# Attention with a gated feed-forward block: where the first sequence's loads stand among the next sequence's moments, and which engine empties its value sums

## The chip, the cores and the metric

The kernel runs on one core of one Trainium2 chip. A core has a matrix engine (TensorE, PE in the profile, with its weight loads as PEld), a vector engine (VectorE, DVE), an activation engine (ScalarE, ACT), a general engine (GpSimd, POOL) and a queue engine that issues transfers (SyncE, SP). The metric is the device time of one launch in microseconds (us). Three runs of the kernel before gave 599.13, 599.91 and 601.34 us; the median is 599.91 us.

## The reference, cut to what matters

Eight sequences of 512 positions and 256 features go through a layer norm, then through two branches whose results are multiplied: attention with 16 heads of 16 features, rotary positions and a causal window of 250 positions, and a three-layer network whose weights are only signs.

```python
xn = _layernorm(x, axis=-1)
# attention
proj = xn @ in_proj_w.T                      # q, k, v
q, k = _apply_rope(q, k)
mask = (delta >= 0) & (delta < CONTEXT)      # CONTEXT = 250
scores = einsum('bhtd,bhsd->bhts', q, k) * D ** (-0.5)
attn = softmax(where(mask, scores, finfo.min))
s = einsum('bhts,bhsd->bhtd', attn, v).reshape(B, T, E) @ out_proj_w.T
# feed-forward with weights of +1 and -1
h = relu(s0 * conn(k0, concat([xn, -xn]))) * 2
h = relu(s1 * conn(k1, h)) * 2
g = silu(s2 * conn(k2, h))
x = x + s * g
```

## The kernel before, in words

The program goes through the sequences b = 0 to 7 and overlaps them: while PE works on the network of sequence b, the attention of b and the projections of b + 1 are put between its matmuls. Every piece of work has a planned place, a number in a planner's time in which each sequence has 42 units (`SEQ = 42.0`). The pieces are sorted by that number and issued in that order (`run`, line 234); a piece can return follow-ups with a delay. The order is then fixed: each engine carries out its instructions in just this order. The same holds for SP: a transfer whose condition is not met holds up every transfer behind it.

The pieces that the change and the prediction touch:

- **Queries and keys to DRAM.** After projection and rotation, `split_hi` and `split_lo` (lines 431 and 437) write a high and a low part of keys and queries to the DRAM tiles `dk` and `dq` (`to_dram`, line 427). Each part is 512 KB and is written twice.
- **Stacks.** `stack(b, g)` (line 444) reads them back for one group g of four heads (g = 0 to 3): four loads of 256 KB, `k` pair 0, `q` pair 0, `k` pair 1, `q` pair 1 (line 450). Loads of `q` need all writes of `dq` to have landed.
- **Moments of the next sequence.** Means and scales of the 512 positions of b + 1 are computed on DVE and POOL (`stats`, line 253), turned by DVE and written to a small DRAM tile `d` by four transfers of 1 KB (`lay_down`, line 289). `load_xT` (line 281) loads the transposed input, 512 KB. `lay_over` (line 298) reads `d` back, broadcast to all 128 partitions, as `of_all`, 512 KB; it can only be issued when the four small writes have landed. `norm_turned` (line 309) then normalises the transposed input in four DVE instructions, two for each half c, and the projection `ka` (line 381) of b + 1 needs its result, the first half of `ka` the half c = 0, the second c = 1.
- **Attention steps.** Two groups take three steps (0 to 2 for groups 0 and 1, 3 to 5 for groups 2 and 3). `step` issues twelve score matmuls into six PSUM banks `sc` (line 746), then the value matmuls of the step before into `po` (line 828), and lets ACT take the exponentials `p` (line 771) and POOL mask them (lines 791 and 798). Step 0 uses group 0 alone: four matmuls with the loads of pair 0, then four with pair 1, then four with both. Step 1 needs group 1 as well, from its third matmul on; pair 1 of group 1 from its seventh.
- **Value sums.** When a group is done, `keep` (line 839) takes its sums out of PSUM: twice for an even group (`V` with a mask, and `S`, both ACT), twice for an odd group (both DVE). There is a single `po` buffer, so the next group's first value matmul waits for this.

In `attention`, the place of the stacks of groups 0 and 1 is fixed relative to `first`, the planned start of the attention, 24.7 for sequence 0. Before, both groups stand at 24.7 - 7.6 = 17.1. The moments of sequence 1 stand at 16.9 (`lay_down`), 17.15 (`load_xT`) and 17.2 (`lay_over`).

Of the kernel before, what the change touches and what calls it, by code (L numbers as in the profile page):

```python
# [16 lines left out]
ALU = mybir.AluOpType  # L17
# [17 lines left out]
def tile_attention_times_gated_ffn(  # L35
# [42 lines left out]
    nc = tc.nc  # L78
# [42 lines left out]
    first_half, second_half = s_sb[:, 3:4], s_sb[:, 4:5]  # L121
# [322 lines left out]
    def stack(b, g):  # L444
        st = states[b]
        for pair in range(2):
            for what in "kq":
                t = stacks.tile([P, T], F32R, tag=f"{what}{pair}", name=f"{what}_{b}_{g}_{pair}")
                rows = st["dram", what][ds(32 * g + 16 * pair, 16)]
                nc.sync.dma_start(t.bitcast(F32), rows.rearrange("p n t -> (p n) t"))  # L450
                st[what, g, pair] = t
# [358 lines left out]
    def values(b, i, tiles):  # L810

        st = states[b]
        blocks = [(*x[:4], tiles, *x[4:]) for x in steps[i]]
        g = over[0][0] if over else blocks[0][0]
        assert over or i == 0 or st["group"] == g or blocks[0][1:3] == (0, 0)
        now = [x for x in over + blocks if x[0] == g]
        now.sort(key=lambda x: x[1:3] != (0, 0))
        if not now:
            return
        over[:] = [x for x in blocks if x[0] != g]  # L820
        if now[0][1:3] == (0, 0):
            st["po"] = ps_o.tile([P, T], F32, tag="po", name=f"po_{b}_{g}")
            st["group"] = g
        po = st["po"]
        done = i >= used[g][-1]
        for k, (_, j, first, n, tiles_, y, off) in enumerate(now):
            for r in range(4):
                nc.tensor.matmul(  # L828
                    po[32 * r : 32 * r + 32, ds(j * P + first, n)],
                    v_columns(j, g, r),  # L830
                    place(tiles_, r, y, off, n),
                    start=(j == 0),
                    stop=(done and k == len(now) - 1),
                    skip_group_check=True,
                )
        if done:
            return [(0.0, lambda: keep(b, g, po))]

    def keep(b, g, po):

        st = states[b]
        odd = g % 2
        S = st["S", g] = outs.tile([P, T], F32, tag="S", name=f"S_{b}_{g}", bufs=3)
        if odd:
            V = st["V", g // 2]
            nc.vector.scalar_tensor_tensor(V, po, second_half, V, ALU.mult, ALU.add)
            nc.vector.tensor_copy(S, po)
        else:
            V = st["V", g // 2] = outs.tile(
                [P, T], F32, tag=f"V{g // 2}", name=f"V_{b}_{g}", bufs=2  # L850
            )
            nc.scalar.mul(V, po, first_half)
            nc.scalar.copy(S, po)

    def flush():
        if pending:
# [4 lines left out]
    def step(b, i):  # L861
        sc = scores(b, i)
        had = len(pending)
        more = flush() or []
        tiles, exps, rest = exponentials(b, i, sc)
        pending.append((rest, (b, i, tiles)))
        return [(-1.4 if had else 0.0, exps)] + more

    def attention(b, among):

        first, end = SEQ * b + (24.7 if b == 0 else 0.0), ends_at(b)
        inside = sorted((at, cost) for at, cost, _ in among if first <= at < end)
        whole = sum(cost for _, cost in inside)
        times, done = [], 0.0
        places = {}
        for at, cost in inside:
            if at in quick or b == 0 and at not in inner:
                places[at] = done
            done += cost
        for n in range(len(steps)):  # L880
            at = min(places, key=lambda at: abs(places[at] * len(steps) - whole * n))
            del places[at]
            times.append(at - 0.01)
        out = []
        for n in range(len(steps)):
            out.append((times[n], 2.5, lambda n=n: step(b, n)))
        for g in range(NG):

            at = times[used[g - 2][-1]] + 0.01 if g > 1 else first - (
                7.6 if b == 0 else 4.0 if b == 1 else 9.0  # L890
            )
            if b and g == 3:
                at += 5.0
            if b and g == 1:
                at = first + 0.01
            out.append((at, 0, lambda g=g: stack(b, g)))
        if b + 1 == B:
            out.append((end, 0.7, flush))
        return out

    def ends_at(b):
        return SEQ * b + (33.0 if b + 1 == B else SEQ)
# [158 lines left out]
    for b in range(B):  # L1061
# [4 lines left out]
        for t in range(NT):  # L1066
            if b + 1 < B:
                at = SEQ * b + 1.5 if b else 2.0
                everything.append((at + t, 0, lambda b=b, t=t: load_x(b + 1, t)))
        everything += divisions(b) + finish(b, b + 1 == B)  # L1070
    for b in range(B):
        everything += attention(b, everything)
# [54 lines left out]
    with tc.If(found < n_rows, label="general"):  # L1127
        for b in range(B):
            for t in range(NT):
                load_x(b, t)  # L1130
            run(prepare(b, plain=True))
            plain_ffn(b)
            for u in range(len(outputs(b))):
                run(finish_ffn(b, u, "at once"))
            for g in range(NG):
                stack(b, g)
                po = ps_o.tile([P, T], F32, tag="po", name=f"f_po_{b}_{g}")
                for t in range(NT):
                    for r in range(4):
                        shifted(b, g, t, r, po)  # L1140
                keep(b, g, po)
                if g % 2:
                    run(divisions(b, (g // 2,)))
            run(finish(b))
# [59 lines left out]
```

## Time and profile before

| what | value |
| --- | --- |
| median of three runs | 599.91 us (599.13 to 601.34) |
| time of the profiled execution | 598.2 us |
| its span, first to last instruction | 596.5 us |
| mean granted TensorE clock | 0.999 |
| PE busy | 584.8 us, 98% of the span |
| DVE, ACT, POOL busy | 333.7, 303.0, 269.9 us (56, 51, 45%) |
| matmuls of the network, L511, share of the chain that ended last | 44% |
| all PE work in that chain | 88% |

The profile is read from PE. The chain of work that ended last is PE work for 88% of the span, so the time is the sum of the matmuls and of the short gaps between them. A gap in PE's timeline that no later wait swallows is a part of the time; everything on another engine counts only where PE, or something that ends in PE, waits for it.

Before the attention of sequence 0 starts, some 37 us into the span, the program loads weights, normalises sequence 0 and sends its keys and queries through DRAM.

### The profile page before, as it was taken

The page shows a single profiled execution, that of the slowest core. Times are in us where ns is not written, and L with a number is a line of the kernel's source. Part 1 is how long each engine was busy: PE and PEld are TensorE (multiplying, and loading weights), DVE is VectorE, ACT ScalarE, POOL GpSimd, SP SyncE. Part 2 cuts the span into 40 slices and gives each one's busy share as a digit, 9 for nine tenths or more (in the row PEclk, how much of TensorE's full clock was granted, in tenths as well). Part 3 has the DMA queues.
Part 4 walks back from the last instruction along what each step waited for, and adds up shares of the span by engine and source line. Part 5 has one row for each costly group of instructions (what it writes and reads, how often), then busy time and mean ns, then how long its engine had stood idle before and what let it go on. Part 6 is the DMA issues. An engine that isn't in the chain of part 4 may idle for free.

```text
span 596.5 us, 10410 instructions
## 1 busy us (share of the span) xinstructions
PE 584.8 (98%) x3788; PEld 364.7 (61%) x3788; DVE 333.7 (56%) x578; ACT 303.0 (51%) x571; POOL 269.9 (45%) x474
## 2 busy tenths in 40 slices
PE   7999999999999999999999999999999999999996
PEld 6655565655655556555566556665566555657785
DVE  6936335666346754478436684366744666427256
ACT  4747564545464545536454465544644645465422
POOL 2736533436334552445444355333652437435513
PEclk9999999999999999999999999999999999999999
DMA  9764844337432474415654075441673335441111
GB/s 277 283 234 143 294 152 127 108 141 250 146 117 98 170 240 133 147 65 223 208 165 154 2 293 189 130 142 65 238 228 113 107 135 208 158 143 43 35 28 53
DMA packets 50086, 92.24 MB, mean 155 GB/s; under 512 B 10992, under 2 KB 18672, under 8 KB 50032
## 3 DMA queue, kind: packets, MB, share of 16 engines
q1 hardware_dynamic: 47600, 89.31, 44.1%
q10 hardware_dynamic: 2432, 2.23, 1.2%
q8 instruction: 31, 0.51, 0.3%
q14 instruction: 23, 0.19, 0.1%
HBM read 53.22 MB, written 38.30 MB: 153 GB/s over the span
## 4 chain that ended last, share of the span: by engine, by line
PE 88%; DVE 3%; DMA 3%; ACT 2%; SPq 1%; POOL 1%; issue 1%; DVEq 0%; POOLq 0%; ACTq 0%
PE h_ps L511 44%; PE po L828 11%; PE z_ps L562 9%; PE sc L746 7%; PE v_ps L361 4%; PE att_ps L962 4%; PE ka_ps L381 2%; PE qb_ps L381 2%; PE qa_ps L381 2%; PE kb_ps L381 2%; DMA of_all<-d 1%; DMA dq<-m_qa 1%; PE warm L232 1%; SPq L450 1%; DMA dk<-kh 1%
## 5 line engine op out<-in xcount | busy, mean ns | idle before, releaser
L771 ACT ACTIVATE p<-sc 128x512 f32<-128x512 f32 (+2 forms) x288 | 150.2, 607 | 57.6 <-PE sc L746 57.4
L791 POOL TENSOR_SCALAR_AFFINE_SELECT p<-p 128x256 f32<-128x256 f32 (+1 forms) x224 | 104.8, 479 | 123.1 <-ACT p L771 105.4
L511 PE MATMUL h_ps<-h1l,w_sb 128*128 128x512 f32 (+1 forms) x576 | 145.3, 394 | 0.0
L511 PE MATMUL h_ps<-h1h,w_sb 128*128 128x512 f16 (+1 forms) x576 | 123.1, 356 | 0.0
L511 PEld LDWEIGHTS h_ps<-h1l,w_sb 128*128 128x128 f32 x576 | 100.4, 188 | 27.4 <-issue 5.7
L511 PEld LDWEIGHTS <-w_sb 128*128 128x128 f16 x704 | 61.3, 98 | 86.3 <-issue 41.5
L522 ACT ACTIVATE h2h<-h_ps 128x512 f16<-128x512 f32 (+1 forms) x72 | 39.6, 550 | 133.1 <-PE h_ps L511 133.1
L520 DVE SCALAR_TENSOR_TENSOR h2l<-h_ps,h2h 128x512 fp32r<-128x512 f32 (+1 forms) x72 | 44.8, 622 | 93.9 <-ACT h2h L522 93.4
L828 PE MATMUL po<-p,v_pad 128*32 128x378 f32 (+4 forms) x1152 | 71.5, 380 | 0.0
L520 DVE SCALAR_TENSOR_TENSOR h1l<-h_ps,h1h 128x512 fp32r<-128x512 f32 x64 | 43.2, 688 | 45.3 <-ACT h1h L522 45.1
L798 POOL TENSOR_SCALAR_AFFINE_SELECT p<-p 128x256 f32<-128x256 f32 x144 | 57.5, 399 | 0.3 <-POOL p L791 0.3
L746 PEld LDWEIGHTS sc<-q,k 64*128 64x128 f32 x576 | 41.9, 186 | 25.0 <-issue 15.1
L633 DVE RECIPROCAL den<-den 128x256 f32<-128x256 f32 (+1 forms) x32 | 52.4, 1641 | 3.7 <-ACT den L628 3.7
L746 PE MATMUL sc<-q,k 64*128 64x378 f32 (+4 forms) x576 | 52.2, 310 | 2.2 <-ACT p L771 1.2
L522 ACT ACTIVATE h1h<-h_ps 128x512 f16<-128x512 f32 x64 | 37.6, 603 | 30.0 <-PE h_ps L511 30.0
L511 PE MATMUL h_ps<-xl,w_sb 128*128 128x512 f32 x128 | 52.3, 489 | 0.0
L952 POOL TENSOR_TENSOR V<-V,R 128x512 f32<-128x512 f32 x16 | 21.2, 1327 | 52.4 <-DVE R L951 52.4
L828 PEld LDWEIGHTS po<-p,v_pad 128*32 128x32 f32 x1152 | 30.7, 109 | 21.2 <-issue 12.0
L991 POOL TENSOR_TENSOR gate<-gate,xr 128x512 f32<-128x512 f32 (+1 forms) x15 | 18.6, 1242 | 47.6 <-DVE gate L984 26.6
L418 POOL TENSOR_TENSOR m_qa<-m_qa,m_qb 128x512 f32<-128x512 f32 x16 | 21.1, 1343 | 38.5 <-DVE m_qb L397 38.5
L511 PE MATMUL h_ps<-xh,w_sb 128*128 128x512 f16 x128 | 38.5, 383 | 0.0
L562 PE MATMUL z_ps<-h2l,w_sb 128*128 128x512 f32 (+1 forms) x144 | 35.6, 389 | 0.0
(102 smaller groups left out, 656.9 us busy)
## 6 DMA issues: line engine op xcount, KB each, us to landing
k<-dk SPq DMA_DIRECT2D x64, 256.0 KB
q<-dq SPq DMA_DIRECT2D x64, 256.0 KB
dk<-kh SPq DMA_DIRECT2D x16, 512.0 KB
dk<-m_ka SPq DMA_DIRECT2D x16, 512.0 KB
dq<-qh SPq DMA_DIRECT2D x16, 512.0 KB
dq<-m_qa SPq DMA_DIRECT2D x16, 512.0 KB
x<-in_x_dram SPq DMA_DIRECT2D x30, 128.0 KB
xT<-in_x_t_dram SPq DMA_DIRECT2D x7, 512.0 KB
```

Source lines behind the costliest of these rows:

```text
L361: nc.tensor.matmul(v.rearrange("p n s d -> p (n s d)"), st["xT"][:, c, ts(t, P)], wqkv_sb[:, c, 2 * E :], start=(c == 0), stop=(c == EC - 1),)
L381: nc.tensor.matmul(ps[:, cols], wqkv_sb[:, c, ds(col, P)], st["xT"][:, c, cols], start=(c == 0), stop=(c == EC - 1),)
L511: nc.tensor.matmul(ph, weights(w, p, c, ts(f, P)), st[src + p][:, c, cols], start=(k == 0), stop=(k == n - 1),)
L520: nc.vector.scalar_tensor_tensor(lo, ph, 0.0, hi, ALU.max, ALU.subtract)
L522: high = lambda: nc.scalar.activation(hi, ph, AF.Relu)
L562: nc.tensor.matmul(pz, weights(w2, p, c, ts(f, P)), st["h2" + p][:, c, cols], start=(c == 0 and p == "h"), stop=(c == NF1 - 1 and p == "l"),)
L633: nc.vector.reciprocal(part, part)
L746: nc.tensor.matmul(sc[r + (4 if y else 2 * pair)][:, ds(at, n)], st["k", g, pair][row, ts(j, P)], st["q", g, pair][row, ds(j * P + first, n)],
L771: nc.scalar.activation(p, s_, AF.Exp, scale=D ** -0.5)
L791: nc.gpsimd.affine_select(out=block, in_=block, compare_op=ALU.is_ge, fill=0.0, base=0, pattern=[[0, heads], [1, P]], channel_multiplier=-1,)
L798: nc.gpsimd.affine_select(out=block, in_=block, compare_op=ALU.is_ge, fill=0.0, base=-1, pattern=[[0, heads], [-1, beyond]], channel_multi ...
L828: nc.tensor.matmul(po[32 * r : 32 * r + 32, ds(j * P + first, n)], v_columns(j, g, r), place(tiles_, r, y, off, n), start=(j == 0), stop=( ...
```

## The change

Two edits, both for sequence 0 alone. In `attention`, the stacks of group 0 move from 17.1 to 24.7 - 7.9 = 16.8, and those of group 1 to 16.8 + 0.5 = 17.3. In `keep`, the two instructions that take an even group out of PSUM are written by DVE in place of ACT; there are two even groups in a sequence, 0 and 2. Nothing is computed differently.

```diff
@@ -849,8 +849,12 @@
             V = st["V", g // 2] = outs.tile(
                 [P, T], F32, tag=f"V{g // 2}", name=f"V_{b}_{g}", bufs=2
             )
-            nc.scalar.mul(V, po, first_half)
-            nc.scalar.copy(S, po)
+            if b == 0:
+                nc.vector.tensor_scalar(V, po, first_half, None, ALU.mult)
+                nc.vector.tensor_copy(S, po)
+            else:
+                nc.scalar.mul(V, po, first_half)
+                nc.scalar.copy(S, po)
 
@@ -887,12 +891,12 @@
             at = times[used[g - 2][-1]] + 0.01 if g > 1 else first - (
-                7.6 if b == 0 else 4.0 if b == 1 else 9.0
+                7.9 if b == 0 else 4.0 if b == 1 else 9.0
             )
             if b and g == 3:
                 at += 5.0
-            if b and g == 1:
-                at = first + 0.01
+            if g == 1:
+                at = first + 0.01 if b else at + 0.5
             out.append((at, 0, lambda g=g: stack(b, g)))
```

On SP the order of these transfers was: four writes of `d`, four loads of group 0, four loads of group 1, `xT`, `of_all`. It becomes: four loads of group 0, four writes of `d`, `xT`, `of_all`, four loads of group 1. The orders of PE and POOL are as before; ACT has four instructions fewer, DVE four more, each pair on DVE standing between two instructions that were there before (the first between line 397 of `m_kb` and line 441 of `m_ka`, the second between two of line 520). Sequences 1 to 7 keep their order on every engine.

## The prediction

> **What bounds the kernel now.** I read first the waits of PE over the whole span, since PE is busy for 98% of it. An engine, its line, whom it waited for, us in total, times, longest:
>
> ```profile
> PE sc L746 <- ACT p L771: 1.2, 1, 1.2
> PE sc L746 <- DMA q<-dq: 1.0, 1, 1.0
> PE ka_ps L381 <- ACT xT L344: 0.5, 1, 0.5
> PE z_ps L562 <- ACT h2h L522: 0.4, 1, 0.4
> PE ka_ps L381 <- DVE xT L309: 0.2, 1, 0.2
> ```
>
> Beside these there is only a start-up wait of 2.8 us. So no change in transfers can win more than a few us. The next view is PE's timeline where the first and the last of these lie (start, length, instruction, idle time before):
>
> ```profile
> 37.56 0.50 PE L746 MATMUL sc<-q,k 64*128 64x378 f32 x4
> 39.26 0.79 PE L746 MATMUL sc<-q,k 64*128 64x378 f32 x8 [1.20 <-ACT p L771]
> 39.98 1.90 PE L511 MATMUL h_ps<-h1h,w_sb 128*128 128x512 f16 x8
> ...
> 43.66 1.08 PE L746 MATMUL sc<-q,k 64*128 64x378 f32 x12
> 44.67 1.49 PE L828 MATMUL po<-p,v_pad 128*32 128x378 f32 x24
> 46.21 1.10 PE L381 MATMUL ka_ps<-xT,wqkv_sb 128*128 128x512 f32 x2
> 47.50 1.12 PE L381 MATMUL ka_ps<-xT,wqkv_sb 128*128 128x512 f32 x2 [0.19 <-DVE xT L309]
> ```
>
> This is sequence 0: step 0 stops after four of its twelve matmuls, and `ka` of sequence 1 stops between its halves. Third, SP's timeline before it:
>
> ```profile
> 26.37 1.28 SPq L427 DMA_DIRECT2D dq<-m_qa  x2
> 31.85 1.33 SPq L289 DMA_DIRECT2D d<-moments  x4
> 33.23 0.35 SPq L450 DMA_DIRECT2D k<-dk  x1
> ...
> 37.00 0.38 SPq L281 DMA_DIRECT2D xT<-in_x_t_dram  x1
> 37.43 0.60 SPq L298 DMA_DIRECT2D of_all<-d  x1
> ```
>
> The stacks stand behind d, which SP can't issue before the moments are turned at 31.82. In between the transfer engines are nearly idle: the stretches of half a microsecond show 393 GB/s to 30.5, then 49 GB/s and less until bytes of the stacks flow from 34.25 on.
>
> The 1.2 us are put down to ACT, which I don't believe. The exponentials that ended at 39.23 read the two banks that the first four matmuls filled; the fifth goes to a third bank, whose former user ended by 26.9 (the copy of v, L368). In the compiled order this matmul also waits for pair 1 of group 0, whose q was issued at 34.58. Landing at 39.2 would be 4.6 us after its issue; four loads of group 1 press in behind it. The lines below show 3.35 us for a like load.
>
> **The change part by part.**
>
> *Stacks of group 0 earlier.* When dq has landed comes from the next sequence, where q is held up by just that:
>
> ```profile
> 74.71 0.32 SPq L450 DMA_DIRECT2D q<-dq  x1
> 75.08 0.42 SPq L450 DMA_DIRECT2D k<-dk  x1
> 75.55 0.43 SPq L450 DMA_DIRECT2D q<-dq  x1
> 76.02 1.58 SPq L918 DMA_DIRECT2D dsums<-S  x2
> 79.21 0.34 SPq L926 DMA_DIRECT2D sums<-dsums  x1
> ```
>
> The chain of waits has dq<-m_qa landing at 74.64 there, some 0.65 us after its last bytes (about 74.0, the rest being the first k). In sequence 0 the last bytes pass at 30.55, so dq lands at 31.2. Bounds: not before 30.55, not after 33.69, when q was issued without a wait. I take 31.2, as its row is the same transfer. The first k needs dk alone and goes out at once behind dq. Then q, k, q at 31.2, 31.6 and 32.0; the last lands 3.35 us (78.90 less 75.55) to 4.66 us (above) later, at 35.4 to 36.7. Step 0 needs it at 37.8, so its wait is gone. Without it the twelve matmuls take 1.00 us (43.66 to 44.67) instead of 2.42 (37.56 to 39.98): 1.42 us. But h_ps of f = 3 takes the bank that the first exponential frees, which ends at 38.73, against 38.56 for the last score; with some 0.06 us of signalling PE goes on at 38.8. **Gain 1.18 us**, and step 1 begins at 42.48.
>
> *d, xT and of_all behind the stacks.* d follows at 32.5 (four issues in 1.33 us, to 33.8). The nearest row for a small write behind three stack loads is dsums above: 79.14 less 74.71, that is 4.43 us after the first q. So d lands at 35.6. The bound from below is the d of sequence 2, where of_all follows 1.30 us after d's last issue with the engines quiet (35.1); from above, 1.9 us more, treated under the rivals. xT goes out meanwhile, at 33.9. SP holds at of_all until 35.7 instead of issuing it at 37.43. The price of of_all with four stack loads right behind it:
>
> ```profile
> 105.67 0.35 SPq L298 DMA_DIRECT2D of_all<-d  x1
> ```
>
> ```profile
> 110.39 3.54 DVE L309 TENSOR_TENSOR xT<-xT,of_all 128x512 f32<-128x512 f32 x4 [0.44 <-DMA of_all<-d]
> ```
>
> 4.7 us, so 40.4; before, with 2 MB ahead, 7.14 us (44.57). Even those 7.14 give 42.8. For `ka` at 44.9 (42.48 + 1.01 + 1.43 for po) the first half needs of_all at 43.5 (two DVE instructions of 0.7 each) and the second at 43.0 (2.75 us for four). So `ka` runs on: before, its halves stood 1.29 us apart and the whole took 2.25 us (46.21 to 48.46), while qa and qb take 1.81; po before it took 1.54 against 1.43 elsewhere. **Gain 0.44 + 0.11 = 0.55 us.** The moved xT and of_all cost SP only their issue times.
>
> *Stacks of group 1 behind of_all.* This is the part that costs. They go out at 36.1 to 38.0 instead of 35.05 to 36.9, behind of_all. In sequence 2 the last bytes of of_all and its four stacks passed at 112.4, 6.7 us after the issue; with 0.65 for the landing, 7.3 us. From 35.7 that is 43.0. Step 1 needs its last pair at its seventh matmul, 0.58 us in (1768 of 3048 columns in 1.00 us), at 43.06. Nothing is left over, and 0.5 MB of xT runs just ahead. By 4.66 us after the last issue at 37.6 it would be 42.3. Bounds 0 and 1.0 us; I take 0.2 late. **Loss 0.2 us.** Behind them on SP stand the stacks of group 2, which wait for step 1 in any case (44.16 before).
>
> *Even groups on DVE.* Added: two pairs, by the rows of L846 and L847 (0.75 and 0.68), or L600 (0.75), 1.43 us each. The first comes when po is done (52.1 before) into DVE's idle 4.04 us before m_ka L441, the second (73.9) into 4.75 us before h2l at 78.30. These stretches hide them; without that cover, m_ka or h2l would be up to 1.43 us later, and next the banks of step 3 or 6. The next group's po starts at 58.4, against DVE's end at about 53.6. Removed: 0.69 + 0.58 and 0.71 + 0.62 us of ACT. ACT then reaches kh sooner, but kh waits for POOL's m_ka (54.68); after the second pair, h2h waits for PE. **0 either way.** POOL beside it: its masks of 0.41 us stay 0.41 beside L846 (60.64).
>
> [...] The rows show 0.75 and 0.68 against 0.69 and 0.58. [...]
>
> [...]
>
> **The sum:** 1.18 + 0.55 - 0.2 = 1.5 us. Everything after is PE's own work, and the dq of sequence 1 hangs on PE (h2h, qh, m_qa after h_ps of f = 5), so it moves along and its 1.0 us stays. The profiled execution takes 598.2 us, 596.5 of span and 1.7 around it: 596.7. The median stood 1.7 above that execution: 599.9 - 1.5 = **598.4 us**.
>
> **The rivals.**
>
> *The step-0 wait is not the load's (0.09).* If an ACT release holds the fifth matmul, the 1.18 us stay and 0.55 less nothing remains: 599.4 us. For it, the profile names ACT; against it, the bank.
>
> *A new wait takes its place (0.22).* Group 1 lands 1 us or more late and step 1 stops where step 0 did. For it, the 43.0 against 43.06 and xT's 0.5 MB (1.3 us at 400 GB/s), which no row has in front. PE then keeps 1.73 - 1.3 = 0.4: 599.5 us; up to no change.
>
> *SP is held at of_all (0.11), the slower side.* If dq lands near its late bound, d goes out after 34.6 and lands after 37.5, and of_all and group 1 with it: 37.5 + 7.3 = 44.8, which is 43.06 + 1.73. From there each us is a us lost. At the bound (dq at 33.69, 2.5 late) d lands at 38.1 and group 1 at 45.5: 0.7 slower, **600.6 us**. Against it, the bytes that end at 30.55.
>
> **How the numbers follow.** The forecast has 0.58, with 597.9 (all of 1.73 and the last 0.24 at h_ps) to 599.1 (0.8) as its own range. The runs before lie up to 0.8 below and 1.4 above their median. I widen by 0.8 below, 597.1, and above to the slower case, 600.9. A measurement can't tell less than 0.5%, 3.0 us, from no change; no term here reaches it. Faster by more needs 1.5 us of luck on the forecast: 0.08. Slower by more needs the last rival and 2.3 us beyond it: 0.05. Same: 0.87.
>
> **What would show it.** q of group 0 issued near 31.2; step 0 in one run of twelve, without a gap; of_all issued near 35.7 and DVE's L309 at some 40.4 without ka waiting; step 1 at 42.5, with a short stop or none at its third or seventh matmul; V and S on DVE at about 50.5 and 72.4; everything from step 2 on earlier by the same 1.5 us. It is wrong if step 0 still stops, if SP's d comes after 34, or if a stop over 1 us appears in step 1.

## The result, and the profile after

The changed kernel takes **601.59 us** (median of 22 executions, 599.0 to 604.6). The kernel before, in the same comparison, takes 599.27 us (22 executions, 597.41 to 603.22). The ratio is **1.0038, with a 95% interval of 1.0022 to 1.0054**: 2.3 us slower. This is less than the 0.5% that the prediction set as its bound, but the interval leaves out 1. The profiled execution of the changed kernel takes 603.17 us, 1.6 above its median, with a span of 601.5 and a mean granted TensorE clock of 0.994; that of before had 598.2, 596.5 and 0.999. So it shows more than the typical loss, and what is typical has to come from the runs below. The profile of before is of an execution 1.1 below its median (598.2 against 599.27), so a difference of two profiles holds for these two executions alone.

The longest of PE's waits over the whole span, after (engine and line, whom it waited for, us in total, times, longest):

```profile
PE sc L746 <- DMA q<-dq: 4.6, 3, 2.1
```

Before, score matmuls waited 1.2 and 1.0 us. Now they wait three times and 4.6 us, each time for a `q` stack. The wait of `ka` for L309 is gone. PE's timeline shows where the three waits lie (start, length, instruction, idle time before):

```profile
37.31 1.07 PE L746 MATMUL sc<-q,k 64*128 64x378 f32 x12
38.55 1.89 PE L511 MATMUL h_ps<-h1h,w_sb 128*128 128x512 f16 x8 [0.17 <-ACT p L771]
...
42.24 0.44 PE L746 MATMUL sc<-q,k 64*128 64x378 f32 x2
44.48 0.66 PE L746 MATMUL sc<-q,k 64*128 64x128 f32 x4 [1.81 <-DMA q<-dq]
45.81 1.01 PE L746 MATMUL sc<-q,k 64*128 64x128 f32 x6 [0.66 <-DMA q<-dq]
46.75 2.77 PE L828 MATMUL po<-p,v_pad 128*32 128x378 f32 x24
49.44 3.04 PE L381 MATMUL ka_ps<-xT,wqkv_sb 128*128 128x512 f32 x4
```

Step 0 runs in one piece of twelve, as intended. Step 1 stops before its third matmul (pair 0 of group 1) and before its seventh (pair 1). But the stops are not all: behind them 24 value matmuls take 2.7 us instead of 1.5, and `ka` takes 2.9 instead of 2.25 (`kb` starts at 52.32), with nothing that they wait for. The windows of the same execution say why. The columns are the stretch and its length, then busy time and count of PE, PEld, DVE, ACT and POOL, then the granted PE clock, the DMA share and GB/s:

```profile
44.00:45.00 1.00, 0.52 (x4) 0.33 (x4) 0.96 (x2) 0.19 (x1) 0.00 (x0) 0.89 1.01 344
...
46.00:48.00 2.00, 2.00 (x14) 0.92 (x18) 1.61 (x3) 2.00 (x6) 0.83 (x2) 0.50 0.87 269
...
51.00:52.00 1.00, 1.00 (x3) 0.45 (x2) 0.00 (x0) 0.00 (x0) 0.00 (x0) 0.70 0.00 0
```

The third number from the end, the clock, is the one to read. 0.89 in the first window means half rate for its last 0.22 us. So from 44.78 on, 0.3 us after the stop of 1.81 us, the granted clock is 0.50, and it stays there until 51.6 (0.70 in the window from 51.00). That is 6.8 us at half rate, or 3.4 us of PE's work. From start to start, the 5.0 us between the two spans are made up so:

| stretch on PE | before, us | after, us | difference |
| --- | --- | --- | --- |
| all up to step 0 | 37.56 | 37.31 | -0.25 |
| step 0 of sequence 0 | 2.42 | 1.24 | -1.18 |
| step 1 | 1.01 | 4.51 | +3.50 |
| po | 1.54 | 2.69 | +1.15 |
| `ka` | 2.25 | 2.88 | +0.63 |
| step 0 of sequence 1 | 2.29 | 3.33 | +1.04 |
| sum | | | +4.89 |

In step 1, 2.47 us are stops and 1.0 us is ordinary work, so 1.04 is the halved clock; po and `ka` lose 1.26 and 1.07 by it against the 1.43 and 1.81 that they take undisturbed. Together 3.4 us of the 4.9 are the clock, and 1.04 is a longer stop in sequence 1, which turns out not to be the change's. Without these two the profile shows half a us of loss.

What is late is seen on SP's timeline, after:

```profile
32.57 0.32 SPq L450 DMA_DIRECT2D q<-dq  x1
...
33.88 1.36 SPq L289 DMA_DIRECT2D d<-moments  x4
35.34 0.41 SPq L281 DMA_DIRECT2D xT<-in_x_t_dram  x1
37.42 0.34 SPq L298 DMA_DIRECT2D of_all<-d  x1
37.82 0.42 SPq L450 DMA_DIRECT2D k<-dk  x1
...
39.23 0.66 SPq L450 DMA_DIRECT2D q<-dq  x1
```

SP is held twice: at the first `q` until 32.57 (dq has landed) and at of_all until 37.42 (d has landed). Group 1 follows of_all and goes out from 37.82 to 39.89. Its pairs let PE go on at 44.48 and 45.81.

### The profile page after: what moved, and what is told of

It reads as the page before. It is cut to its first block, busy times and chain, and to the rows that moved or that the text cites. A ratio compares the mean times of both kernels' runs of the same rounds, so it can differ in the third digit from the quotient of the medians.

```text
span 601.5 us, 10407 instructions
## 1 busy us (share of the span) xinstructions
PE 587.4 (98%) x3788; PEld 365.7 (61%) x3788; DVE 336.8 (56%) x582; ACT 300.5 (50%) x567; POOL 270.9 (45%) x474
## 4 chain that ended last, share of the span: by engine, by line
PE 89%; DMA 4%; DVE 3%; ACT 2%; POOL 1%; issue 1%; SPq 1%; POOLq 0%; DVEq 0%; ACTq 0%
PE h_ps L511 44%; PE po L828 11%; PE z_ps L562 9%; PE sc L746 7%; PE v_ps L361 4%; PE att_ps L966 4%; PE ka_ps L381 2%; PE qb_ps L381 2%; PE qa_ps L381 2%; PE kb_ps L381 2%; DMA q<-dq 2%; DMA dq<-m_qa 1%; PE warm L232 1%; DMA dk<-kh 1%; DVE m_qa L441 1%
## 5 line engine op out<-in xcount | busy, mean ns | idle before, releaser
L828 PE MATMUL po<-p,v_pad 128*32 128x378 f32 (+4 forms) x1152 | 72.8, 386 | 0.0
L956 POOL TENSOR_TENSOR V<-V,R 128x512 f32<-128x512 f32 x16 | 22.6, 1411 | 53.5 <-DVE R L955 53.5
L418 POOL TENSOR_TENSOR m_ka<-m_ka,m_kb 128x512 f32<-128x512 f32 x16 | 20.0, 1270 | 37.5 <-DVE m_kb L397 32.8
```

What stands on the lines that cost most here:

```text
L418: nc.gpsimd.tensor_tensor(m[:, i], m[:, i], n[:, i], op)
L828: nc.tensor.matmul(po[32 * r : 32 * r + 32, ds(j * P + first, n)], v_columns(j, g, r), place(tiles_, r, y, off, n), start=(j == 0), stop=( ...
```

## The experiments

The edits are in `attention`, in `keep` and, once, in the planner's table of places; they are shown against the changed kernel unless said otherwise. In the table, n is the number of executions; the ratio is to executions of before in the same comparison; the comparisons ran on several chips, so medians of different ones are compared only roughly. The last columns count executions by their mean granted clock. A stretch of 3.4 us at half rate takes 0.003 off that mean. In the fourteen profiles the last 0.3 to 3.2 us of the span (0.97 in that of before, 0.31 in the changed kernel's), where PE has no work left, are at half rate too, which costs no time but takes up to 0.0027 off. So 0.998 and more is an execution without such a stretch, 0.995 and less one with at least one, and 0.996 and 0.997 can be either.

| kernel | n | median, us | ratio (95%) | 0.998 and more | 0.995 and less |
| --- | --- | --- | --- | --- | --- |
| changed kernel | 22 | 601.59 | 1.0038 (1.0022 to 1.0054) | 5 | 13 |
| before, beside the first runs | 32 | 599.35 | | 18 | 4 |
| order_alone | 9 | 602.30 | 1.0047 (1.0028 to 1.0065) | 2 | 6 |
| dve_alone | 12 | 598.87 | 0.9988 (0.9970 to 1.0005) | 7 | 0 |
| fill_wait | 12 | 600.31 | 1.0018 (0.9999 to 1.0037) | 6 | 3 |
| second_before_xt | 12 | 599.29 | 1.0003 (0.9988 to 1.0018) | 6 | 4 |
| fill_short | 12 | 600.75 | 1.0020 (1.0001 to 1.0039) | 7 | 4 |
| both_ahead | 12 | 601.01 | 1.0033 (1.0018 to 1.0048) | 2 | 4 |
| second_behind_alone | 12 | 600.54 | 1.0008 (0.9986 to 1.0030) | 5 | 4 |
| xt_first | 12 | 598.59 | 0.9991 (0.9969 to 1.0014) | 8 | 4 |
| xt_first_again | 12 | 598.39 | 0.9975 (0.9957 to 0.9993) | 3 | 7 |
| two_fills | 12 | 600.02 | 1.0000 (0.9984 to 1.0016) | 10 | 0 |
| xt_first_fill | 9 | 596.89 | 0.9946 (0.9929 to 0.9964) | 5 | 0 |
| before_fill | 12 | 599.25 | 1.0002 (0.9987 to 1.0016) | 7 | 1 |

Beside the later runs, 10 of 78 executions of before are at 0.995 or less; together with the 4 of 32 that is 14 of 110.

The mean also misses one thing, at the start. The same four matmuls, in the profiles of before and of two_fills:

```profile
8.54 1.13 PE L381 MATMUL ka_ps<-xT,wqkv_sb 128*128 128x256 f32 x4 [0.46 <-ACT xT L344]
```

```profile
8.47 2.07 PE L381 MATMUL ka_ps<-xT,wqkv_sb 128*128 128x256 f32 x4 [0.47 <-ACT xT L344]
```

In two of the fourteen profiles, two_fills and fill_short, these take twice as long, and the second half of `ka` comes 1.9 and 1.8 us later than before. No edit reaches these matmuls. The clock record of two_fills begins only at 12.5 us (that of before at 8.4), so its mean is still 1.000, while this execution is the slowest of its twelve (601.73).

**The order alone** (order_alone): the value sums stay on ACT.

```diff
-            if b == 0:
-                nc.vector.tensor_scalar(V, po, first_half, None, ALU.mult)
-                nc.vector.tensor_copy(S, po)
-            else:
-                nc.scalar.mul(V, po, first_half)
-                nc.scalar.copy(S, po)
+            nc.scalar.mul(V, po, first_half)
+            nc.scalar.copy(S, po)
```

> The changed kernel with the even groups written by ACT again, so that only the order of the transfers is changed. Theory A (the loads of group 1 land late at 44.4 and 45.7 us, PE stops in step 1, and after the stop the clock is halved for some 7 us): as the changed kernel, 2 to 3 us slower than before (about 601.6), step 1 with a stop of 1.8 us or more. Rival D (the even groups on DVE cost the time): back at the time before, within 0.5 us.

**The engine alone** (dve_alone): the places of before, with the DVE branch of `keep`.

```diff
-                7.9 if b == 0 else 4.0 if b == 1 else 9.0
+                7.6 if b == 0 else 4.0 if b == 1 else 9.0
...
-            if g == 1:
-                at = first + 0.01 if b else at + 0.5
+            if b and g == 1:
+                at = first + 0.01
```

> The kernel before with the even groups of sequence 0 written by DVE, the order of the transfers unchanged. Theory A: no difference from before (within 0.5 us), PE's waits as before (1.2 us in step 0, 0.2 in ka, 1.0 in sequence 1). Rival D: 2 us slower than before, with a wait on DVE in PE's list.

The order alone gives 1.0047, the whole loss; the engine alone 0.9988, with 1 inside its interval. So the loss belongs to the order. One sign of rival D is there all the same: in the profile of dve_alone PE does wait for DVE, for 0.76 us. DVE's and PE's timelines:

```profile
55.73 2.70 DVE L441 TENSOR_TENSOR m_ka<-m_ka,kh 128x1024 fp32r<-128x1024 f32 x1 [2.22 <-ACT kh L434]
```

```profile
59.09 0.50 PE L746 MATMUL sc<-q,k 64*128 64x256 f32 x3 [0.76 <-DVE h2l L520]
```

In before this `m_ka` starts at 55.80 and takes 1.39 us, and a mask of POOL beside it 1.39 in place of 0.41; here `m_ka` takes 2.70 and no mask is long. So it isn't started later by the two new instructions. It is as long in three of the eleven profiles with the even groups on DVE (dve_alone, second_before_xt, xt_first_again), where PE waits 0.76, 0.75 us and not at all, and in none of the three without. Three are too few to say whether the move to DVE makes it more frequent; over twelve executions it costs nothing that can be measured.

The profiled execution of order_alone adds something. PE's timeline there:

```profile
44.23 0.55 PE L746 MATMUL sc<-q,k 64*128 64x128 f32 x4 [1.62 <-DMA q<-dq]
45.62 0.61 PE L746 MATMUL sc<-q,k 64*128 64x128 f32 x6 [0.83 <-DMA q<-dq]
46.16 1.50 PE L828 MATMUL po<-p,v_pad 128*32 128x378 f32 x24
47.59 1.98 PE L381 MATMUL ka_ps<-xT,wqkv_sb 128*128 128x512 f32 x4
```

The stops are there, 1.62 and 0.83 us, but po and `ka` run at their usual 1.43 and 1.82 us from start to start, and the mean clock is 0.999. With stops and without half rate the span is 597.6, 1.1 over that of before. So both profiles of this order without a filler have the stops, and only one of them the half rate; by their mean clock of 0.995 or less, 6 of 9 executions here have it somewhere.

**The stop, covered** (fill_wait): 13 matmuls on the identity, with no use, are put on PE ahead of step 1.

```diff
+        if b == 0:
+            out.append((times[1] - 0.002, 0, lambda: warm(13)))
```

> The changed kernel with 13 matmuls of the identity (26 instructions, about 3 us at full clock) put on PE right ahead of step 1; they write nothing that is read, and PE works where it waited. Theory A with the clock lost to the stop: the loads land as late as in the changed kernel, but the granted clock stays at 1.0 and the value matmuls and ka that follow take 1.5 and 1.9 us again instead of 2.7 and 2.9; 2 to 3 us less than the changed kernel, 599 us or a little under. Rival C (the clock falls for another reason than the stop): still half clock near 45 to 52 us and no gain.

**A shorter cover** (fill_short): the same with `warm(9)`.

> The changed kernel with 9 identity matmuls (18 instructions, about 2.1 us) on PE ahead of step 1, so that PE works through most of the stop and is done when the first load of group 1 lands. Theory A: fewer executions with a mean clock of 0.995 or less than the 13 of 22 of the changed kernel (3 of 12 or fewer, as with the longer filler), no half-clock stretch between 44 and 52 us in the profile, and a time between the undisturbed and the mean time of the changed kernel: 600 to 600.5 us. Rival C: half or more of the executions at 0.995 or less, 601.6 us.

PE's timeline of fill_wait:

```profile
41.95 3.06 PE L232 MATMUL warm<-ident 128*128 128x128 f32 x26
...
45.54 0.55 PE L746 MATMUL sc<-q,k 64*128 64x128 f32 x4 [0.16 <-DMA q<-dq]
46.87 0.62 PE L746 MATMUL sc<-q,k 64*128 64x128 f32 x6 [0.78 <-DMA q<-dq]
47.41 1.49 PE L828 MATMUL po<-p,v_pad 128*32 128x378 f32 x24
48.84 1.98 PE L381 MATMUL ka_ps<-xT,wqkv_sb 128*128 128x512 f32 x4
```

The filler occupies PE while the loads fly, so group 1 is no earlier and step 1 still ends late. But po and `ka` take 1.43 and 1.82, and half rate is rarer: 3 of 12 instead of 13 of 22. The median is about 1.3 us below the changed kernel's (600.31 against 601.59), though PE does 3.06 us more work; I had expected more, 599 or a little under, and the intervals of the two ratios overlap. This speaks for a loss in two parts, the late loads and the clock; two_fills, below, says it more clearly. The shorter filler gives 600.75, which the intervals don't tell from the longer one. Its profile has no half rate at step 1, but has it elsewhere, in the timeline and then the windows:

```profile
82.76 0.79 PE L746 MATMUL sc<-q,k 64*128 64x378 f32 x8 [1.42 <-DMA q<-dq]
```

```profile
84.00:86.00 2.00, 2.00 (x29) 1.27 (x24) 0.00 (x0) 0.40 (x1) 1.13 (x3) 0.50 0.67 143
86.00:88.00 2.00, 2.00 (x20) 0.89 (x11) 0.87 (x2) 0.00 (x0) 0.00 (x0) 0.66 0.72 248
```

This is the stop in step 0 of sequence 1, which the kernel before has too. A stop of 1.42 us there was enough for 3.4 us of half rate. In the changed kernel's profile the same stop is 2.10 us long and the clock stays. So the length of a stop doesn't decide alone. Nor do the single profiles show that the change sets its size: those with the order of before have 0.97 and 1.92 (dve_alone), others 1.04 (fill_wait), 1.13 (order_alone) and 1.31 (xt_first).

**Other orders.** If the queue is what is late, it matters what stands behind the wait for d. Four orders of SP's transfers after the first `k`, of which the changed kernel's is: group 0, d, xT, of_all, group 1.

second_before_xt (group 0, d, group 1, xT, of_all):

```diff
-                at = first + 0.01 if b else at + 0.5
+                at = first + 0.01 if b else at + 0.15
```

> The changed kernel with the loads of group 1 put between d and xT: group 0, d, group 1, xT, of_all. Theory A: group 1 is issued at about 35.3 to 37.2 without waiting for d and lands by 42, so step 1 doesn't stop and the clock holds; of_all lands near 44.6 as before, and ka, which PE reaches 1.2 us earlier than before, waits some 1.6 us for it: what step 0 gains is given back there, about the time before (599.3, within 1 us), 2 us less than the changed kernel. If the stops in step 1 are not what costs, it stays near 601.6.

both_ahead (group 0, group 1, d, xT, of_all):

```diff
-                at = first + 0.01 if b else at + 0.5
+                at = first + 0.01 if b else at + 0.01
```

> The changed kernel with both groups' loads ahead of the moments: group 0, group 1, d, xT, of_all. Theory A: d lands near 39.5 behind 2 MB of loads and SP stops at of_all until then; of_all lands near 44 to 45; step 0 and step 1 don't stop, ka waits 1 to 2 us for of_all: about the time before, 599 to 600 us. If it were the second group's place alone that costs and the way of d cost nothing, 597.7 us.

second_behind_alone (d, group 0, xT, of_all, group 1), that is the place of group 1 alone, with the even groups on DVE:

```diff
-                7.9 if b == 0 else 4.0 if b == 1 else 9.0
+                7.6 if b == 0 else 4.0 if b == 1 else 9.0
...
-                at = first + 0.01 if b else at + 0.5
+                at = first + 0.01 if b else at + 0.2
```

> The kernel before's d, then group 0, then xT, of_all, and group 1 last; even groups on DVE as in the changed kernel. So d isn't behind a load and only group 1 is moved behind of_all. Theory A (SP held at of_all until d lands at 37.4, behind the loads of group 0, makes group 1 late): of_all is issued at about 35.6 without a wait, group 1 at 36 to 37.9, and lands some 1.5 us sooner than in the changed kernel, 43 to 44.3; step 1 stops for 0.5 to 1.2 us, step 0 for less than before: 599 to 600 us. If group 1's place behind of_all is enough by itself, the stop is as long as in the changed kernel (2.5 us) and the time 601 us or more.

With group 1 ahead of xT, step 1 has no stop, and `ka` waits a little for of_all in its stead. PE's timeline of second_before_xt:

```profile
42.61 1.07 PE L746 MATMUL sc<-q,k 64*128 64x378 f32 x12
...
45.81 1.10 PE L381 MATMUL ka_ps<-xT,wqkv_sb 128*128 128x512 f32 x2 [0.71 <-issue]
47.10 1.13 PE L381 MATMUL ka_ps<-xT,wqkv_sb 128*128 128x512 f32 x2 [0.18 <-DVE xT L309]
```

This order is 1.0003, back at the time of before: moving group 1 ahead of of_all takes away the loss. With d last of all, of_all can't leave until 41.72, and `ka` stops (SP's, then PE's timeline of both_ahead):

```profile
41.72 0.34 SPq L298 DMA_DIRECT2D of_all<-d  x1
```

```profile
46.72 1.10 PE L381 MATMUL ka_ps<-xT,wqkv_sb 128*128 128x512 f32 x2 [1.63 <-issue]
```

Its median of 601.01 is more than I expected, and more than this profile explains: the profiled execution took 598.93, the least of its twelve. Part of it fits the clock, for only 2 of 12 executions show 0.998 or more; the rest is open.

With group 1 behind of_all but d still ahead of group 0, PE's timeline of second_behind_alone shows

```profile
43.62 0.55 PE L746 MATMUL sc<-q,k 64*128 64x128 f32 x4 [0.84 <-DMA q<-dq]
44.99 1.01 PE L746 MATMUL sc<-q,k 64*128 64x128 f32 x6 [0.81 <-DMA q<-dq]
45.92 2.62 PE L828 MATMUL po<-p,v_pad 128*32 128x378 f32 x24
```

Here d lands early and of_all goes out at 35.37 without a wait. So of the changed kernel's 2.47 us of stops, 1.65 are there with the place behind of_all and xT alone, and the 0.8 beyond come with SP being held for d. Half rate came here too (po takes 2.55 from start to start), with two stops of only 0.8 us. Its ratio, 1.0008, has too wide an interval to say more.

Step 0 of this run tells something about the other half of the change. SP's, then PE's timeline:

```profile
34.35 0.43 SPq L450 DMA_DIRECT2D q<-dq  x1
```

```profile
37.34 1.40 PE L746 MATMUL sc<-q,k 64*128 64x378 f32 x12
```

The last load of group 0 goes out about when it did before (34.35 against 34.58), and yet step 0 runs in one piece, 1.33 us from start to start instead of 2.42; the three profiles with the order of before stop there for 1.20, 1.16 (dve_alone) and 1.52 us (before_fill). So its late issue alone didn't make the stop of before; with xT and of_all right behind it in place of the loads of group 1, the same load came in time. Moving group 1 alone wins nearly all of the 1.18 us. The move of group 0 ahead of d wins them too (both_ahead, with group 1 right behind, stops for 0.16 us), but it puts d behind these loads, and SP is held for it.

**The best order** (xt_first): xT, which needs nothing, goes ahead of the stacks into the time in which SP waits for dq; group 1 ahead of of_all.

```diff
-                at.update(load=17.15, stats=14, down=16.9, over=17.2, norm=24.8, k=28.1, q=31.6)
+                at.update(load=16.7, stats=14, down=16.9, over=17.2, norm=24.8, k=28.1, q=31.6)
...
-                at = first + 0.01 if b else at + 0.5
+                at = first + 0.01 if b else at + 0.15
```

> A version to beat both: xT (which waits for nothing but its buffer) is issued first, while SP waits for dq, then group 0, d, group 1, of_all. Theory A: the 0.5 MB of xT pass while the transfer engines would be idle; q of group 0 is issued at about 32.5 to 33, group 1 lands by 42, of_all, with 0.5 MB less ahead of it, at about 43; neither step 0, step 1 nor ka stops for more than 0.5 us: 1.0 to 1.7 us less than before, 597.7 to 598.4. If xT ahead holds up dq's last bytes and q of group 0 is issued after 34, step 0 stops again and nothing is won.

SP's and then PE's timeline of xt_first:

```profile
27.56 1.08 SPq L281 DMA_DIRECT2D xT<-in_x_t_dram  x1
...
32.66 0.32 SPq L450 DMA_DIRECT2D q<-dq  x1
...
37.47 0.32 SPq L298 DMA_DIRECT2D of_all<-d  x1
```

```profile
42.31 1.07 PE L746 MATMUL sc<-q,k 64*128 64x378 f32 x12
43.31 1.49 PE L828 MATMUL po<-p,v_pad 128*32 128x378 f32 x24
44.74 1.98 PE L381 MATMUL ka_ps<-xT,wqkv_sb 128*128 128x512 f32 x4
```

of_all leaves when it did in the changed kernel (37.47 against 37.42), but nothing needed sooner stands behind it. Steps 0 and 1, po and `ka` all run without a stop, and the span is 594.8, 1.7 below that of before. But over twelve executions the ratio is 0.9991, and 1 is inside: four executions with a clock of 0.995 or less average 601.21, the others 597.61. I had expected 597.7 to 598.4. The same program once more (xt_first_again):

> The same program as xt_first, for more executions: theory A expects 598 to 599 us median with about a third of the executions at a clock of 0.995 or less, in which it takes 3 us more than in the others.

0.9975, with 1 just outside. Here 7 of 12 are at 0.995 or less, not a third, and they take 1.6 us more than the others (599.06 against 597.50), not 3. With 11 of 24, half rate is more frequent in this order than before (14 of 110), though one stop fewer is left; why is open. That stop is the one of sequence 1 (1.31 and 1.52 us in the two profiles), so it is covered too (xt_first_fill); and both stops of the changed kernel (two_fills):

```diff
+        if b == 1:
+            out.append((times[0] - 0.002, 0, lambda: warm(6)))
```

two_fills has this beside the `warm(13)` of fill_wait.

> xT first as in the run of that name, and 6 identity matmuls ahead of step 0 of sequence 1, the one place where it still stops (1.3 us). Theory A: no more than 1 of 12 executions with a clock of 0.995 or less (4 of 12 without the filler), mean 597.6 to 598, 1.5 to 2 us less than before. Rival C: as without the filler, 4 of 12, mean 598.8.

> The changed kernel with identity matmuls ahead of both stops: 13 ahead of step 1 of sequence 0, 6 (about 1.4 us) ahead of step 0 of sequence 1, which stops for 1 to 2 us in every kernel so far. Theory A (a granted clock of 0.995 or less comes from PE standing still in these two places): at most 1 of 12 executions at 0.995 or less, all within some 2 us, mean near 600. Rival C (the clock falls for other reasons): 3 to 4 of 12 as with one filler.

**xt_first_fill takes 596.89 us, 0.9946 (0.9929 to 0.9964)**, and beats both kernels: its slowest execution, 598.93, is below the fastest of the changed kernel, 599.00. PE's timeline in sequence 1:

```profile
75.58 1.50 PE L232 MATMUL warm<-ident 128*128 128x128 f32 x12
77.01 1.08 PE L746 MATMUL sc<-q,k 64*128 64x378 f32 x12
```

None of its nine executions is at 0.995 or less; nor is any of the twelve of two_fills, which is level with before (1.0000). Without the fillers it was 11 of 24 and 13 of 22. So with these stops filled the clock held. Is the gain of xt_first_fill then the filler's alone? The kernel before with the filler of sequence 1 (before_fill):

```diff
+        if b == 1:
+            out.append((times[0] - 0.002, 0, lambda: warm(6)))
```

> The kernel before with 6 identity matmuls ahead of step 0 of sequence 1 and nothing else changed, to tell what of the best version's gain is the filler's. Theory A: no execution at a clock of 0.995 or less (about one in eight without the filler), mean 599.2 to 599.7, up to 0.5 us less than before: the rest of the gain of xT first with filler, some 2 us, is the order's.

1.0002: no. On the order of before the filler gains nothing that can be measured. Its profile shows what remains there, first PE's timeline, then the windows:

```profile
39.18 0.79 PE L746 MATMUL sc<-q,k 64*128 64x378 f32 x8 [1.52 <-DMA q<-dq]
39.91 3.59 PE L511 MATMUL h_ps<-h1h,w_sb 128*128 128x512 f16 x8
```

```profile
39.00:40.00 1.00, 0.82 (x9) 0.71 (x10) 0.00 (x0) 0.31 (x1) 1.00 (x3) 0.97 0.98 358
40.00:41.00 1.00, 1.00 (x3) 0.34 (x4) 0.00 (x0) 1.00 (x3) 0.21 (x2) 0.50 1.00 375
...
43.00:44.00 1.00, 1.00 (x5) 0.81 (x4) 0.00 (x0) 0.00 (x0) 0.00 (x0) 0.82 0.27 107
```

The stop in step 0 of sequence 0, the one that the change was to remove, can itself cost half rate for some 3.4 us; eight matmuls of the network then take 3.0 us instead of 1.5. And here the profile names the stack as what ended this stop, not ACT. The order of xt_first removes this stop, the filler covers the other.

## Why the prediction was wrong, point by point

The prediction was 598.4 us, 1.5 below before; the result is 2.3 above, and outside the range.

- **Step 0, right.** The gain was put at 1.18 us and is 1.18 (2.42 to 1.24), with the foreseen short wait of h_ps (0.17). That the stop hung on the load and not on ACT is confirmed: it is gone with the load earlier. The first rival falls. But an early issue wasn't needed for it: second_behind_alone has nearly the same gain with the old issue times, because group 1's loads are not right behind.
- **dq landed at 32.5, not 31.2.** This is the first step that failed. I took the end of the writes from the windows of before, where the large flow ends at 30.5, and counted what follows as nothing. The windows of before show it plainly:

```profile
30.00:30.50 0.50, 0.50 (x3) 0.12 (x2) 0.41 (x3) 0.03 (x1) 0.00 (x0) 1.00 1.02 393
30.50:31.00 0.50, 0.50 (x4) 0.26 (x3) 0.17 (x2) 0.50 (x2) 0.44 (x1) 1.00 0.14 49
31.00:31.50 0.50, 0.50 (x4) 0.23 (x3) 0.00 (x0) 0.50 (x2) 0.50 (x1) 1.00 0.06 25
...
32.00:32.50 0.50, 0.50 (x4) 0.41 (x3) 0.50 (x2) 0.19 (x1) 0.50 (x1) 1.00 0.04 16
```

  The last column is GB/s: 49, 25, then 33 in the window left out, then 16, so a trickle lasts until 32.5, and `q` goes out at 32.57, 32.36 and 32.23 in three profiles with this order (some 1.5 us later in fill_short and two_fills, which lost 1.8 and 1.9 us at the start). The column before it is the busy share of the 16 transfer engines; 0.06 is one of them. The packets in the trace agree: from 30.72 to 32.44 those of 4 KB go strictly one behind the other, and of the 16 packets of 4 bytes that end the last write, 15 lie between 30.56 and 30.73 and one at 32.44. After the change that one is at 32.19, and `q` goes out 0.38 us behind it. One engine is late, and SP's hold ends with it, not with the bulk. Sequence 1, from which I took the row, could not show this: there the 16 come within 0.42 us (73.87 to 74.29).
- **d and of_all, 1.7 us late.** d was put 4.43 us after the first `q` and landed 4.8 after it, so its row held; the start was wrong. of_all left at 37.42 instead of 35.7 and its data released DVE's L309 at 42.95, 5.5 us later, not 4.7. `ka` had that much to spare, and its wait is gone as predicted; the 0.55 us is hidden in this profile by the half clock, but po and `ka` without a wait are seen in order_alone.
- **Group 1, the term that was mis-sized.** I put its landing 7.3 us after of_all's issue, at 43.0, with a loss of 0.2 us and 1.0 at most. It let PE go on at 45.81, 8.4 us after that issue, and the stops are 2.47 us. The late d is not the larger part: in second_behind_alone of_all goes out at 35.37 without a wait, pair 1 still lets PE go on only at 44.99, 9.6 us later (there group 0 goes out later too), and 1.65 us of stops remain. So the 7.3 us are the term that failed; their row, in sequence 2, had nothing in flight ahead (8 GB/s or less from 102 to 106 us), and here xT and more were. The third rival described just this path and its landing (45.5 at the bound), but I gave it 0.11, for the bytes that "end" at 30.55.
- **The clock, missing.** That rival said that from its bound on each us late is a us lost, which gives 600.6. It isn't so here: after some of PE's stops a further 1.7 or 3.4 us were lost to the granted clock, which was 0.50 for 3.4 us (fill_short, before_fill, second_behind_alone) or 6.8 us (the changed kernel). Among executions at 0.998 and more, the changed kernel averages 600.40 us (5, from 599.0 to 601.73) and before 599.16 (18 of the 32, of another comparison), 1.2 apart; over all executions the means are 601.76 and 599.66, 2.1 apart. So, as a rough estimate, some 1.2 us of the loss are the late loads less the gains, and about 0.9 is half rate that comes more often. No step of the prediction and no rival contained it.
- **The stop in sequence 1** "moves along and stays": its place does, but its length varies from 0.97 to 2.10 between profiles, with no order to it that I can see.
- **Even groups on DVE: 0, right by the time.** L853 and L854 took 0.75 and 0.68 us as priced, nobody waited for them, and dve_alone can't be told from before. The wait of 0.76 us that its profile shows was not foreseen: the prediction has `m_ka` and h2l late only if the new instructions push them, and here `m_ka` began on time and ran long.

Shown by runs: that the order makes the loss (order_alone, dve_alone), that it is gone when group 1 goes ahead of xT and of_all (second_before_xt), and that half rate comes with PE's stops and all but goes when fillers cover them (two_fills, xt_first_fill). How the loss divides between late loads and clock is an estimate. Still open: why one transfer engine is late with dq, what decides which stop drops the clock, and why both_ahead, without the stops in step 1, is nearly as slow as the changed kernel.

## What to carry to other kernels

Before a late load is moved ahead, look at what goes out right behind it; to move that away can be enough, as in second_behind_alone, where step 0 took 1.33 us instead of 2.42 with the load issued about when it was before (34.35 against 34.58). Where a queue issues in order, as SP did here (held at of_all until 37.42 us, the loads of group 1 from 37.82 on), look at each wait and at what stands behind it: loads that need nothing go ahead of the wait, into its idle time, and a load with a near deadline never stands behind a load that waits for a tiny write. Price a stop of the matrix engine at more than its length, for here the clock fell to 0.50 for 3.4 or 6.8 us after some of them; where a stop can't be removed, matmuls with no use can be cheaper than idling (a ratio of 0.9946 with them in xt_first_fill, 0.9991 and 0.9975 without). Read when a transfer lands from the last bytes that move, however few, and not from the end of the main flow: here one of the sixteen engines was done with dq at 32.44 us, the others by 30.73.

## What the runs showed of the hardware

The granted clock fell to 0.50 after stops of 1.42 (sequence 1 of fill_short), 1.52 (before_fill), 1.62 (sequence 1 of second_behind_alone) and 1.81 us (the changed kernel), and once within the second of two of 0.84 and 0.81 us (second_behind_alone), for 3.4 us each or, in the changed kernel's profile, 6.8. Stops of 1.52 (xt_first_again), 1.62 (order_alone), 1.92 (dve_alone) and 2.10 us (sequence 1 of the changed kernel) passed without it. So the length of a stop doesn't tell by itself whether the clock falls, and no run shows what does.
